# Keys and values of two groups by seven products, and transfers by one queue, in an attention and feed-forward kernel

## The chip, the cores and the metric

The kernel runs on one core of a Trainium2 chip. The core has five engines that work in parallel, each through its own list of instructions in order: PE (matrix products; its weight loads are shown apart as PEld), DVE (vector work), ACT (scalar functions and copies), POOL (general work) and SP (which here only issues transfers). SP, ACT and POOL can each issue DMA transfers. The metric is the device time of one execution in microseconds (us); lower is better. A profile is one execution recorded by the hardware.

## The reference

The input x has 1024 rows of 512. All arithmetic is float32. Two layers are computed, each as x + layernorm(f(layernorm(x))):

```python
# f of layer 1: causal attention, 32 query heads in 8 groups, head size 128
q = (xn @ w_q).reshape(B, S, 8, 4, 128)      # w_q: 512 x 4096
k = (xn @ w_k).reshape(B, S, 8, 128)         # w_k: 512 x 1024
v = (xn @ w_v).reshape(B, S, 8, 128)         # w_v: 512 x 1024
scores = einsum(q, k) * 128 ** -0.5          # causal mask
attn = softmax(scores) @ v                   # per head
out = attn.reshape(B, S, 4096) @ w_o         # w_o: 4096 x 512
# f of layer 2: a dense 512 x 512 product with bias, plus 8 low-rank experts (rank 16)
# weighted by a softmax router with 15 outputs
```

## The kernel before

**Tiling.** Group g has one key head, one value head and four query heads. A row t is 128 of the 1024 positions. A block (g, t) is one row of one group; its scores are four tiles of 128 lines, 4 heads x 32 positions each (`NSUB` is 4), against all positions up to its own. There are 64 blocks. The first 48 go group by group through rows 0 to 7. The last 16 alternate between groups 6 and 7 in pairs of rows 0-1, 6-7, 4-5, 2-3, so that a row's attention is complete there and its second layer can begin. In the text, (2..5, 2) means row 2 of groups 2 to 5, and (1, 3, 5; 7) row 7 of groups 1, 3 and 5. An index u counts pairs of rows (256 positions).

**One turn of the main loop (`for i in range(N)`)** does the following for block i:

- `loads(i)` issues weight loads that later blocks need. Before the change ACT issues them.
- For each of the four score tiles, `scores` runs one or two matmuls into a PSUM tile (`s`, two buffers), then mask (L519), maximum (L521) and exp with row sum (L526). One tile later follow the reciprocal (L532) and the scaling of the probabilities (L533), and then a DVE transpose of 32 x 32 pieces into `T` (L539).
- After the fourth tile `to_keys` moves `T` into `K` by 16 transfers, which put positions on partitions. By the remainder of a count by three, 11 go to SP and 5 to POOL.
- Between the tiles `run_share` spreads the block's other PE work: the query projection of a later pair of rows (odd i), key and value projections (`other`), `attend(i - 2)`, which multiplies the probabilities in `K` with the values (`po`), and for even i the output projection of an earlier pair of rows (`project_o_pair`: products a to e, then DVE accumulates at L640). `weave` mixes two lists in proportion to their columns. What stands first in a list runs first.

So block i's probabilities are transposed early in turn i + 1, transferred, and used in turn i + 2.

**Keys and values.** `project_k(g, qb)` computes 128 x 512 keys by four matmuls of 512 columns, and ACT evicts them with the factor `scale` (L359). It runs at rows 2 and 6. `project_v(gv, t)` computes the values of two groups for one row by four matmuls of 256 columns, ACT evicts them (L344), and it runs at every row of even groups.

**Seven products.** From the third pair of rows on the query projection (`project_q_halves`) and the output projection use a scheme after Strassen and Winograd: of a product of 2 x 2 blocks it needs seven block products instead of eight, on sums of the operands. `combine_q` makes the sums of the weights and `combine_x` those of xn, on POOL. A PSUM bank holds two to four products; `merge` adds banks into the result, one ACT copy and then DVE additions (L418). PSUM has three banks (`bank`) for all projections.

**Buffers that matter.** `wq` has one buffer, `wk`, `wv` and `wo` have two, `po` has one bank, attnT (the attended rows, evicted by ACT at L565) has three.

**The end.** After the loop the last rows are ordered by hand: `project_o_pair` of the last pair of group 6, `attend` and `project_o` of the last two blocks, and for the rows c, d, e, f the router and feed-forward pieces (`out_x[0]` and `out_x[2]` hold two base products each, `out_x[1]` a transpose, `out_x[3]` the last product). DVE's and ACT's order there is fixed by `go`.

Most instructions are marked to keep their place on their engine; the others (the merges among them) are placed by the scheduler. All matmuls carry the line of one helper (L102), all kept transfers that of another (L108), so that they are told apart by their tiles.

Of the kernel before, what the change touches and what calls it, by code (L numbers as in the profile page):

```python
# [15 lines left out]
P = 128  # L16
# [6 lines left out]
def kernel(  # L23
# [15 lines left out]
):  # L39

# [80 lines left out]

    def load_q(g, i, by=nc.scalar):

        if weights.get(("q", i), (None,))[0] == g:
            return
        hw = R * D // 2
        w = wp.tile([P, KC, hw], F32, tag=f"wq{i}", name=f"wq_{g}_{i}", bufs=1)
        load(w, w_q[:, ts(2 * g + i, hw)].rearrange("(c p) n -> p c n", p=P), by)
        weights["q", i] = (g, w)

    def combine_q(m):


        g = pairs[m][0]
        if weights.get("sq", (None,))[0] == g:
            return
        w = [weights["q", i][1] for i in range(2)]
        hk = KC // 2
        a11, a12, a21, a22 = w[0][:, :hk], w[0][:, hk:], w[1][:, :hk], w[1][:, hk:]
        s1, s2, s4 = (  # L140
            ffn.tile([P, hk, 2 * D], F32, tag="hy", name=f"sq_{g}_{n}", bufs=3) for n in range(3)
        )
# [7 lines left out]
        weights["sq", 0] = (a11, a12, s4, a22, s1, s2, a21)  # L150
        weights["sq"] = (g,)

    def combine_x(m):

        u = pairs[m][1]
# [3 lines left out]
        t12, t34 = (ffn.tile([P, 2, hk, P], F32, tag="x", name=f"tx_{m}_{n}") for n in range(2))  # L159
# [3 lines left out]
        weights["tx"] = (b11, b21, b22, t4, t1, t2, t3)  # L163

    def load_v(gv, i, by=nc.scalar):
# [4 lines left out]
        load(w, rows.rearrange("(c p) n -> p c n", p=P), by)  # L170
        for c in range(KC // 2):
            weights["v", gv, i * (KC // 2) + c] = w[:, c, :]
# [167 lines left out]

    def project_v(gv, t):
        def finish(pm):
            v = vs[gv, t] = act.tile([P, GV * D], F32, tag="v", name=f"v_{gv}_{t}", bufs=NT + 2)
# [11 lines left out]

    def project_k(g, qb):
        def finish(pm):
            kT = kTs[g, qb] = act.tile([P, QB], F32, tag="kT", name=f"kT_{g}_{qb}", bufs=2 * NQB)
            nc.scalar.mul(kT, pm, scale)  # L359
# [41 lines left out]

    def project_q_halves(m):
# [14 lines left out]
        def add(dst, src, to):  # L417
            nc.vector.tensor_tensor(dst, src, to, ALU.add)  # L418

        def merge(b):  # L420

            one, two = pm[b][:, 0], pm[b][:, 1]
            if b == 0:
                nc.scalar.copy(both(0), one.unsqueeze(1).to_broadcast([P, 2, NSUB, 2 * SQ]))  # L424
                add(half(0, 0), two, half(0, 0))
            elif b == 1:
                add(half(1, 0), one, half(0, 1))
                add(half(0, 1), two, half(1, 0))
            elif b == 2:
                add(half(1, 1), one, half(0, 1))  # L430
                add(half(1, 0), one, half(1, 0))
                add(half(1, 0), two, half(1, 0))
            else:
                add(half(0, 1), one, half(0, 1))


        order = (0, 1, 5, 6, 4, 2, 3)

        def piece(n, c, k):
            i, b, x = order[n], n // 2, n % 2  # L440
# [5 lines left out]
            assert weights["sq"] == (g,)  # L446
# [15 lines left out]
        ]  # L462

# [38 lines left out]
    def scores(g, t, j):  # L502
# [32 lines left out]
        def finish():  # L535
# [8 lines left out]
            if j == NSUB - 1:  # L544
                to_keys(g, t)
# [3 lines left out]
    def to_keys(g, t, by=(nc.sync, nc.sync, nc.gpsimd)):  # L549
# [9 lines left out]
    def weighted_values(g, t):  # L559


        def finish(po):
            o = act.tile([P, R * P], F32, tag="attnT", name=f"attnT_{g}_{t}", bufs=3)
# [172 lines left out]
    def ffn_out(t):  # L736
# [3 lines left out]
        def base(c):  # L740
            if c == 0:

                if t in (e, f):
# [3 lines left out]
            matmul(pf[0], state["hT", t][:, c, :], weights["base", c], start=(c == 0), stop=False)  # L747
# [23 lines left out]
        w = [(512, lambda c=c: base(c)) for c in range(KC)]  # L771
# [11 lines left out]
    def projections(i):  # L783
# [12 lines left out]
        if i < N2:  # L796
            if t == 2:
                other += project_k(g, 1)
            if t == 6:
# [4 lines left out]
            elif g % GV == 0 and (g or t >= TPB):  # L804
                other += project_v(g // GV, t)
        else:
            n = i - N2
            for k, what in ((0, (G - 1, 0)), (2, (G - 2, 1)), (3, (G - 1, 1))):
                if n == k:
                    other += project_k(*what)  # L810
# [207 lines left out]
```

## Time and profile before

| | |
|---|---|
| Runs | 1077.7, 1077.79, 1078.58 us; median 1077.79 |
| Profiled execution | 1077.89 us, of which the span from the first to the last instruction is 1076.1 |
| Granted clock of PE | 0.996 of full speed |
| Transfers T to K | 11 x 64 on SP, 5 x 64 on POOL |

A line of the groups gives source line, engine, operation, output<-inputs, shape and count; then busy time in us, mean ns of one, and the idle time ahead of them with what ended it. A line of the timeline gives start and duration in us, engine, line, operation and count; a bracket holds the wait before it. A line of the windows gives the stretch, its length, and the busy time and number of instructions of PE, PEld, DVE, ACT and POOL, then the clock and the DMA.

### The profile page before, as it was taken

What the parts mean: (1) busy time and instruction counts of PE and PEld (TensorE: products, weight loads), DVE (VectorE), ACT (ScalarE), POOL (GpSimd) and SP (SyncE); (2) the same over time, 40 slices, a digit from 0 to 9 for tenths busy, and PEclk for the clock granted to TensorE, in tenths of its full rate; (3) what the DMA queues carried; (4) which work ended last, traced back from release to release, by engine and by line L of the source; (5) the groups of instructions that cost most, each with busy time, mean ns of one, the idle gap of its engine ahead of it and who ended that gap; (6) DMA issues with size and microseconds to landing.
All of it is one profiled execution on the core that took longest, in us unless ns stands there. A gap on an engine that the chain in (4) does not pass through costs nothing.

```text
span 1076.1 us, 15090 instructions
## 1 busy us (share of the span) xinstructions
PE 1053.7 (98%) x4398; PEld 708.9 (66%) x4398; DVE 703.5 (65%) x1689; ACT 480.9 (45%) x969; POOL 360.7 (34%) x720
## 2 busy tenths in 40 slices
PE   9999999999999999999999999999999999999995
PEld 7776666667676676766777676756676566466442
DVE  4586657876576657866576666877337676576756
ACT  2654435544354434544354434554235454353411
POOL 2734245243333335332352334332142122232412
PEclk9999999999999999999999999999999999999998
DMA  5244242553135432454124531545334555343221
GB/s 186 50 129 117 69 120 68 161 141 89 33 86 145 94 89 59 128 140 123 33 74 133 127 87 46 141 130 129 77 108 118 159 139 133 108 117 100 69 69 39
DMA packets 74913, 111.96 MB, mean 104 GB/s; under 512 B 18176, under 2 KB 47760, under 8 KB 74832
## 3 DMA queue, kind: packets, MB, share of 16 engines
q1 hardware_dynamic: 38576, 59.29, 21.9%
q0 software_dynamic: 11216, 24.45, 9.2%
q10 hardware_dynamic: 25040, 27.27, 8.0%
q8 instruction: 36, 0.59, 0.2%
q14 instruction: 45, 0.37, 0.1%
HBM read 33.34 MB, written 2.10 MB: 33 GB/s over the span
## 4 chain that ended last, share of the span: by engine, by line
PE 89%; DVE 5%; POOL 2%; DMA 1%; ACT 1%; issue 1%; SPq 1%; POOLq 0%; ACTq 0%; DVEq 0%
PE po L102 21%; PE s L102 21%; PE pq L102 17%; PE pv L102 5%; PE pk L102 5%; PE pa L102 4%; PE pe L102 4%; PE pO L102 2%; PE pb L102 2%; PE pd L102 2%; PE pc L102 2%; PE pf L102 2%; SPq L108 1%; DVE T L539 1%; POOL K L108 1%
## 5 line engine op out<-in xcount | busy, mean ns | idle before, releaser
L533 ACT ACTIVATE p<-p,rec 128x32 f32<-128x32 f32 (+31 forms) x256 | 188.1, 735 | 225.0 <-DVE rec L532 160.4
L102 PE MATMUL po<-K,v 128*128 128x512 f32 x576 | 279.2, 594 | 2.4 <-DMA K<-T 2.1
L102 PE MATMUL s<-kT,qT 128*128 128x512 f32 (+15 forms) x768 | 272.5, 464 | 3.8 <-ACT attnT L565 2.1
L526 ACT ACTIVATE p<-s,nmax 128x32 f32<-128x32 f32 (+31 forms) x256 | 179.1, 700 | 189.6 <-DVE nmax L521 180.6
L108 POOL DMA_DIRECT2D K<-T x320 | 157.9, 500 | 265.0 <-DVE s L519 55.1
L539 DVE STREAM_TRANSPOSE T<-p 128x128 f32<-128x128 f32 (+7 forms) x256 | 197.6, 773 | 64.8 <-ACT p L533 54.2
L102 PEld LDWEIGHTS s<-kT,qT 128*128 128x128 f32 x768 | 141.4, 190 | 127.1 <-issue 107.2
L521 DVE TENSOR_REDUCE nmax<-s 128x1 f32<-128x32 f32 (+31 forms) x256 | 180.6, 705 | 7.7
L102 PEld LDWEIGHTS po<-K,v 128*128 128x128 f32 x576 | 104.8, 190 | 64.3 <-issue 54.1
L519 DVE TENSOR_TENSOR s<-s,smask 128x32 f32<-128x32 f32 x256 | 48.2, 188 | 112.5 <-PE s L102 112.0
L102 PE MATMUL pq<-xnT,wq 128*128 128x128 f32 (+1 forms) x656 | 113.8, 321 | 0.0
L102 PEld LDWEIGHTS pq<-xnT,wq 128*128 128x128 f32 x656 | 100.6, 191 | 14.7 <-issue 7.7
L524 POOL MEMSET p<- 128x96 f32 (+2 forms) x192 | 29.9, 161 | 235.6 <-DVE T L539 198.0
L418 DVE TENSOR_TENSOR qT<-pq,qT 128x256 f32<-128x256 f32 x161 | 63.4, 413 | 34.8 <-ACT qT L424 27.2
L102 PE MATMUL pv<-wv,xnT 128*128 128x256 f32 x256 | 71.2, 381 | 0.5 <-ACT xnT L293 0.5
L565 ACT COPY attnT<-po 128x512 f32<-128x512 f32 x64 | 37.3, 582 | 66.7 <-PE po L102 66.4
L102 PE MATMUL pk<-xnT,wk 128*128 128x512 f32 x128 | 64.5, 593 | 0.0
L102 PE MATMUL pa<-wo,attnT 128*128 128x256 f32 x224 | 61.8, 385 | 0.0
L162 POOL TENSOR_TENSOR tx<-xnT 128x256 f32<-128x256 f32 x46 | 33.4, 726 | 81.1 <-PE pq L102 74.3
L102 PEld LDWEIGHTS pq<-tx,wq 128*128 128x128 f32 x368 | 49.6, 192 | 9.1 <-issue 7.7
L102 PEld LDWEIGHTS pq<-tx,sq 128*128 128x128 f32 x368 | 49.8, 192 | 8.6 <-issue 8.3
L102 PEld LDWEIGHTS pa<-wo,attnT 128*128 128x128 f32 x224 | 41.2, 190 | 19.2 <-issue 14.3
(121 smaller groups left out, 1165.1 us busy)
## 6 DMA issues: line engine op xcount, KB each, us to landing
wq<-in_w_q_dram ACTq DMA_DIRECT2D x27, 512.0 KB, 5.0
K<-T SPq DMA_DIRECT2D x88, 128.0 KB, 3.6
K<-T SPq DMA_DIRECT2D x88, 112.0 KB, 3.3
K<-T SPq DMA_DIRECT2D x88, 96.0 KB, 2.6
wo<-in_w_o_dram ACTq DMA_DIRECT2D x28, 256.0 KB, 3.9
K<-T SPq DMA_DIRECT2D x88, 80.0 KB, 2.7
K<-T SPq DMA_DIRECT2D x88, 64.0 KB, 2.2
K<-T POOLq DMA_DIRECT2D x40, 128.0 KB, 4.6
```

Source lines behind the costliest of these rows:

```text
L102: keep(nc.tensor.matmul(*args, **kw))
L108: keep(by.dma_start(dst, src))
L162: nc.gpsimd.tensor_tensor(dst, p, q, ALU.subtract)
L418: nc.vector.tensor_tensor(dst, src, to, ALU.add)
L519: keep(nc.vector.tensor_tensor(s[:, n - SQ : n], s[:, n - SQ : n], smask, ALU.add))
L521: keep(nc.vector.tensor_reduce(nmax, s[:, :n], AX.X, ALU.max, negate=True))
L524: nc.gpsimd.memset(p[:, n:full], 0.0)
L526: keep(nc.scalar.activation(p[:, :n], s[:, :n], AF.Exp, bias=nmax, accum_out=total))
L533: keep(nc.scalar.mul(p[:, :n], p[:, :n], rec))
L539: nc.vector.transpose(turned[g, t][:, :, j, :, :].rearrange("p b k q -> p k b q"), p[:, :full].rearrange("p (k b q) -> p k b q", b=R, q=SQ),)
L565: copy = nc.scalar.copy(o, po)
```

## The change

- `combine_w` takes the sums out of `combine_q`. `combine_k` and `combine_v` use it for two groups at once, and `project_halves` computes keys and values of groups 2 to 7 by seven products per 256 positions: each product is two matmuls of 128 columns, one bank holds four products, and `merge` has one ACT copy and six DVE additions. Groups 0 and 1 keep the old way. The xn sums of `combine_x` are used by keys, queries and values of the same rows.
- They run in odd turns, keys before the queries and values after. The last three of groups 6 and 7 run in turns 49 to 51, with `combine_x` at the end of the turn before.
- `scale` is multiplied into w_k by ACT (`scale_k`) two rows after it is loaded, instead of into the keys.
- The query products come in the order 0, 1, 5, 6, 3, 2, 4 instead of 0, 1, 5, 6, 4, 2, 3; the last merge is one addition of 512.
- All weight loads in the loop are issued by SP. All 16 transfers of a block are issued by SP, but for the first block, rows 1 to 3 of groups 1, 3 and 5, and the last block, which keep 11 and 5.
- attnT has two buffers. Values of two rows share a tile, keys have four tiles by name.
- At the end `project_o_pair` and the base products of row c come first, then `attend(N - 2)`; `attend(N - 1)` moves behind `project_o(N - 2)`.

```diff
+    def scale_k(g):
+        keep(nc.scalar.mul(weights["k", g], weights["k", g], scale))
...
+    def combine_w(key, parts, sums):
+        (a11, a12, a21, a22), (s1, s2, s4) = parts, sums
         for dst, p, q, op in (
             (s1, a21, a22, ALU.add),
             (s2, s1, a11, ALU.subtract),
...
+        weights[key] = (a11, a12, s4, a22, s1, s2, a21)
...
     def project_k(g, qb):
         def finish(pm):
-            kT = kTs[g, qb] = act.tile([P, QB], F32, tag="kT", name=f"kT_{g}_{qb}", bufs=2 * NQB)
-            nc.scalar.mul(kT, pm, scale)
+            nc.scalar.copy(key_tile(g, qb), pm)
...
+    PRODUCTS = (0, 1, 5, 6, 3, 2, 4)
...
             if b == 0:
-                nc.scalar.copy(both(0), one.unsqueeze(1).to_broadcast([P, 2, NSUB, 2 * SQ]))
+                q = each(0).rearrange("p (e s) n -> p e s n", e=2)
+                nc.scalar.copy(q, one.unsqueeze(1).to_broadcast([P, 2, NSUB, 2 * SQ]))
                 add(half(0, 0), two, half(0, 0))
             elif b == 1:
-                add(half(1, 0), one, half(0, 1))
-                add(half(0, 1), two, half(1, 0))
+                add(half(1, 0), one, half(1, 0))
+                add(half(1, 1), two, half(1, 0))
             elif b == 2:
-                add(half(1, 1), one, half(0, 1))
-                add(half(1, 0), one, half(1, 0))
+                add(half(0, 1), one, half(1, 1))
                 add(half(1, 0), two, half(1, 0))
             else:
-                add(half(0, 1), one, half(0, 1))
-        order = (0, 1, 5, 6, 4, 2, 3)
+                add(both(1), one.unsqueeze(1).to_broadcast([P, 2, NSUB, 2 * SQ]), both(1))
...
+    def project_halves(name, u, sums, product, quarters):
+        hk = KC // 2
+        pm, to = {}, {}
+        def merge(b):
+            c11, c12, c21, c22, first = to[0]
+            p = pm[b]
+            if b == 0:
+                nc.scalar.copy(first, p[:, 0:1, :].to_broadcast([P, 2, P]))
+                add(first, p[:, 1:3, :], first)
+                add(c22, p[:, 3], c12)
+            else:
+                add(c21, p[:, 0], c22)
+                add(c12, p[:, 1], c12)
+                add(c12, p[:, 2], c12)
+                add(c22, p[:, 2], c22)
+        def piece(n, k):
+            i, b = PRODUCTS[n], n // 4
...
+            lhsT, rhs = product(weights[sums][i][:, k, :], weights["tx"][i][:, k, :])
+            matmul(pm[b][:, n % 4, :], lhsT, rhs, start=(k == 0), stop=(k == hk - 1))
+            if k == hk - 1 and n in (3, 6):
+                merge(b)
+        return [(P, lambda n=n, k=k: piece(n, k)) for n in range(7) for k in range(hk)]
...
             if j == NSUB - 1:
-                to_keys(g, t)
+                three = (nc.sync, nc.sync, nc.gpsimd)
+                at = blocks.index((g, t))
+                short = at < 1 or at < N2 and g % 2 and t in (1, 2, 3)
+                alone = not short and at < N - 1
+                to_keys(g, t, by=three[:1] if alone else three)
...
-            o = act.tile([P, R * P], F32, tag="attnT", name=f"attnT_{g}_{t}", bufs=3)
+            o = act.tile([P, R * P], F32, tag="attnT", name=f"attnT_{g}_{t}")
...
+        if i % 2 and m < len(pairs) and n < 0:
+            gm, um = pairs[m]
+            if gm >= first and gm % 2 == 0:
+                q = project_k_halves(gm, um) + q + project_v_halves(gm // GV, um)
...
+        elif 0 < n < NT // 2:
+            q = project_k_halves(G - 2, n) + q
+            other += project_v_halves((G - 2) // GV, n)
         return q, other
     def loads(i):
         g, t = blocks[i]
+        by = nc.sync
...
     rescale_scores()
+    o_pair = project_o_pair(*pairs[N // 2 - 2])
     finish_scores()
...
-    o_pair = project_o_pair(*pairs[N // 2 - 2])
-    run([turn_d] + weave(o_pair[:8], attend(N - 2)) + [products_d] + o_pair[8:])
+    run(o_pair[:8] + out_c[0] + out_c[2] + o_pair[8:16] + [turn_d] + o_pair[16:])
+    run(attend(N - 2) + [products_d])
     go(d)
-    run(out_c[0] + out_c[1] + out_c[2] + attend(N - 1))
-    run(project_o(*blocks[N - 2]))
+    run(out_c[1] + project_o(*blocks[N - 2]))
     go(e)
     run(out_c[3])
     go(e, e)
-    run(project_o(*blocks[N - 1]))
+    run(attend(N - 1) + project_o(*blocks[N - 1]))
```

## The prediction

> **What bounds the kernel.** The page's first two parts come first: one engine is busy almost throughout, and the chain that ended last runs through it.
>
> ```profile
> PE 1053.7 (98%) x4398; PEld 708.9 (66%) x4398; DVE 703.5 (65%) x1689; ACT 480.9 (45%) x969; POOL 360.7 (34%) x720
> ...
> PE 89%; DVE 5%; POOL 2%; DMA 1%; ACT 1%; issue 1%; SPq 1%; POOLq 0%; ACTq 0%; DVEq 0%
> ```
>
> So a microsecond of PE work is worth a microsecond, wherever PE does not begin to wait instead. Next, the groups by shape: the key and value projections that the change replaces, the query products that are already done in seven parts, and two DVE additions that resemble the new ones.
>
> ```profile
> L102 PE MATMUL pv<-wv,xnT 128*128 128x256 f32 x256 | 71.2, 381 | 0.5 <-ACT xnT L293 0.5
> L102 PE MATMUL pk<-xnT,wk 128*128 128x512 f32 x128 | 64.5, 593 | 0.0
> L102 PE MATMUL pq<-tx,wq 128*128 128x128 f32 x368 | 53.3, 275 | 0.0
> L418 DVE TENSOR_TENSOR qT<-pq,qT 128x256 f32<-128x256 f32 x161 | 63.4, 413 | 34.8 <-ACT qT L424 27.2 <-PE pq L102 6.2
> L726 DVE TENSOR_TENSOR hw<-pl,w 128x128 f32<-128x128 f32 x8 | 2.3, 289 | 0.2
> ```
>
> Every float32 matmul leaves two records: 4 groups of values x 8 rows x 4 pieces make 128 matmuls and 256 records. I call a record a pass. Passes overlap, so a mean of 381 ns is no price; the price is the step from start to start in the timeline.
>
> ```profile
> 17.38 3.60 PE L102 MATMUL pk<-xnT,wk 128*128 128x512 f32 x8
> 20.81 3.62 PE L102 MATMUL pq<-xnT,wq 128*128 128x256 f32 x16
> ...
> 510.03 1.95 PE L102 MATMUL pq<-xnT,wq 128*128 128x128 f32 x16
> 511.81 1.06 PE L102 MATMUL pq<-tx,sq 128*128 128x128 f32 x8
> ```
>
> 8 passes of 512 columns take 20.81 - 17.38 = 3.43 us, 0.429 each; 16 of 256 take 3.46 (the next group starts at 24.27), 0.216 each; 16 of 128 take 1.78, 0.112 each. The price per column is nearly the same for all three.
>
> **1. The products, on the path.** For a pair of groups the keys were 2 x 2 x 4 = 16 matmuls of 512, 32 passes x 0.429 = 13.73 us; the values 64 passes x 0.216 = 13.82. Both become 4 x 7 x 2 = 56 matmuls of 128, 112 passes x 0.112 = 12.54. A pair saves 1.19 + 1.28 = 2.47 us, three pairs 7.4.
>
> Here a page speaks against the change. The Trainium skill (TensorE: Matmul & The Clock Gate, "Back-to-back issue gap") says that in a stream of weight loads and matmuls the load counts too, and gives about 81 ns for 128 columns against 131 for 512: four short ones would cost 2.5 times one long one. By that ratio 112 short passes cost as much as 112 x 0.429 x 81/131 = 29.7 us where the row says 12.54, and the three pairs would lose some 95 us. The row is float32, of the same shape and in the same place, with a weight load before each pass, so I take 0.112.
>
> **2. Where the work moves.** By counting each block's passes in the instruction order of the changed kernel (a block is a group and a row, a score matmul begins it), blocks (2..5, 2) fall to 9.17 us of PE work, from 12.60 in odd groups and 14.33 in even ones; (2..5, 6) and (1, 6) lose 3.4 to 5.2. Blocks (2, 4; 1, 3, 5) gain 4.5, and (1, 3, 5; 7) gain 6.3. PE's sum stays -7.4, but an engine that was hidden under 12.6 us must now fit into 9.2.
>
> **3. DVE.** A merge of four quarters adds one addition of 256 (0.413) and five of 128 (0.289 each): 1.86 us. 24 merges are 44.6, less 3 for queries (23 x one 256-wide addition, about 0.14 saved when two become one of 512). They stand where PE got 4.5 to 6.3 us more, and are hidden there. The critical block is (3, 2), where DVE has lost nothing:
>
> ```profile
> 407.50:418.60 11.10, 11.10 (x43) 7.61 (x42) 8.44 (x23) 5.79 (x14) 3.53 (x9) 1.00 0.19 48
> ...
> 184.00:197.10 13.10, 13.10 (x55) 9.08 (x54) 11.33 (x33) 6.90 (x13) 2.93 (x8) 1.00 0.41 106
> ```
>
> Columns: length, busy PE, weight loads, DVE, ACT, POOL. DVE's 8.44 against 9.17 is a share of 0.92; the highest that I find without a PE stall is 11.33 of 13.10, 0.865. At 0.865 the block takes 9.8 us: 0.6 lost, in four groups 2.4. From nothing (two score tiles of slack) to 2.4; I take 1.5.
>
> **4. Order of the query products.** In odd groups a score matmul waits for the last query merge (0.9 us at block (g, 3), 0.4 at (g, 5), each three times). The last merge is now 512 wide, 0.69 by the row of the same width (acc<-pd), instead of 0.41: at (g, 5) 0.3 later, three times, +0.9. At (g, 3) two additions after the last product replace three: even. In even groups value products follow and hide it.
>
> **5. Transfers.** SP issues 16 of 16 per block instead of 11; the other five go to POOL in 11 blocks only.
>
> ```profile
> 342.32 0.97 DVE L539 STREAM_TRANSPOSE T<-p 128x768 f32<-128x768 f32 x1
> ...
> 343.36 7.35 SPq L108 DMA_DIRECT2D K<-T  x11
> ...
> 366.92 1.02 PE L102 MATMUL po<-K,v 128*128 128x512 f32 x2
> ...
> 1012.57 21.55 SPq L108 DMA_DIRECT2D K<-T  x22
> ```
>
> This is block (2, 5): transposed at 343.3, 11 transfers issued in 7.35, 0.64 from one to the next where none waits (7.0 in most blocks), used at 366.92: 23.6 us of time. Sixteen need 15 x 0.64 + 2.6 for the last to land (the page's median for 96 KB) = 12.2. But (2, 6) loses 5.2 us, and in (2, 7) the products with K move forward by 6.2 because the four value projections ahead of them in the woven list are gone: 12.2 us remain, no margin. The same count leaves 0.1 at (4, 5), -0.1 at (6, 3), and 1.1 to 1.9 at ten more blocks: (1, 3, 5; 4), (1, 3, 5; 5), (2, 4; 1), (2, 4; 3); 1.7 at (3, 5; 1), which keep three queues; elsewhere over 2. I take +1.0 for three places with none, from 0 to +4.
>
> The second page that bears on it: the Trainium skill (DMA: Bandwidth & Descriptors, "Issuing engines are not separate DMA queues") says that several issuing engines save only the issue time, usually small beside the transfer. By that the five transfers cost SP next to nothing. The row says 0.64 us each, 3.2 us of delay per block, as much as the landing itself (2.6). I count the row.
>
> Weight loads, 71 issues, go from ACT to SP. They stand ahead of the block's transfers, are issued when SP has just done the previous block's, and wait for products already finished: 0.5 us each, four at most, with the transpose still 4 us away. If the cover went, K would be 2 us late. ACT and POOL are freed of about 30 and 130 us, neither on the path: a gain of 0 to 2 (two early stalls of 0.6 and 0.9 with late POOL work near them); I take 0. Scaling w_k: 8 x 0.6 on ACT, well ahead of use; POOL's sums: 36 x 0.73 (24 for weights, 12 for xn), in blocks where it loses nearly as much in transfers; the closest, xn's for block (7, 1), come some 2.2 us after their tile is free and are needed after 2.9. Nothing for both. attnT with two buffers instead of three: its old content is read before the new is copied, nothing.
>
> **6. The end.** PE waits before the last blocks:
>
> ```profile
> 1021.10 1.10 PE L102 MATMUL po<-K,v 128*128 128x512 f32 x2 [1.88 <-DMA K<-T]
> ...
> 1024.22 1.13 PE L102 MATMUL pb<-wot,sums 128*128 128x256 f32 x4 [0.30 <-DVE acc L640]
> ...
> 1028.43 1.25 PE L102 MATMUL pl<-ra_sb,hT 128*128 128x143 f32 x8 [1.36 <-ACT hT L293]
> ```
>
> With waits not bracketed there, 4.9 us in all. The new order puts the output pair first, so K of (7, 2) is in time and hT too. But pb needs DVE's sums, which come at 1022.3 when pa ended at 1019.9: a new wait of 2.4. Then pb, pc 1.75, base products 3.43, pd, pe 2.6, a transpose 0.45, po 2.6, pl and ptw 1.2, pO 3.4, pf 0.9 lead to 1038.6; K of (7, 3), transposed near 1027.9 behind three accumulations, is there at 1036.8; po 3.4, the copy 0.65, pO 3.4 end at 1046.2 against 1047.4 before. From there the work is unchanged and PE fills it. Gain 1.2; bounds -3.7 (the wait for sums gone) to +1.
>
> **Sum.** -7.4 + 1.5 + 0.9 + 1.0 - 1.2 = -5.2. The profiled execution took 1077.89 us with a span of 1076.1; the median of the runs is 1077.79. Span 1070.9, median **1072.6 us**, 0.5% less.
>
> **Rivals.** (a) SP decides, slower. If one issue costs not 0.64 but 0.80 us (8.7 for 11 at (2, 7), when transfers wait for earlier ones to land), sixteen end 2.4 us later; over the thirteen places the stalls are 13 x 2.4 - 14.9 (sum of the margins) = 16 us, and the time 1072.6 - 1.0 + 16 = 1088. It breaks even at 13x - 14.9 = 6.2, x = 1.6 us or 0.75 per issue. Against it: the slow issues stood beside POOL's transfers, which are gone. (b) DVE paces (g, 2) to (g, 5). At its share over these four blocks in group 3, 41.2 us of 52.1 = 0.79, their length stays as it was, and 2 x 3.4 us of the gain is lost: 1072.6 - 1.5 + 6.9 = 1078. Against it: the 0.865 above. (c) The covers hold, POOL's and ACT's relief takes the early stalls and the sums at the end come in time: -7.4 - 2 - 3.7 + 0.9 = -12.2, 1065.6. (d) That it doesn't do what it says is excluded for counts: the changed order holds 336 short matmuls and 55 transfers on POOL.
>
> **Numbers.** Forecast 0.62, (a) 0.12, (b) 0.12, (c) 0.14. The forecast's own range is 1069 to 1076; with (c) below and (b) above, and the bounds of steps 3 and 5, 1066 to 1079.5. A measurement of this kernel tells 0.2%, 2.2 us, from no change. Faster: 0.58 of the forecast + (c) + a little of (b) = 0.74; same 0.12; slower 0.14.
>
> **What would show it.** Right: pk and pv with 336 passes each of 128 columns beside what is left of the old shapes, in 0.112 steps; PE busy down by about 7; DVE up by some 40. Step 3 shows as waits of PE's s at (g, 2); step 5 as waits of po for DMA K<-T at the thirteen blocks; step 6 as pb waiting for sums near 1020 and no wait for K. It is wrong if those waits sum to more than 6 us, or if passes of 128 step slower than 0.112 where keys and values stand together.

## The result

The changed kernel took 1066.36 us in the median (1065.36 to 1067.22), the kernel before 1078.18 beside it: a ratio of 0.9889, with a 95% interval from 0.9872 to 0.9907, so 11.8 us less in the medians, and 12.0 by the ratio (10.0 to 13.8). The forecast was 1072.6, 5.2 us less: the direction was right, the gain was more than double. Its profiled execution took 1066.64 us with a span of 1064.9, 11.2 less than the span before. The page of after, its lines for the engines, the chain and K's largest transfers:

```profile
PE 1046.5 (98%) x4782; PEld 729.8 (69%) x4782; DVE 740.1 (70%) x1810; ACT 480.7 (45%) x965; POOL 255.0 (24%) x491
...
PE 90%; DVE 3%; SPq 3%; ACT 1%; DMA 1%; issue 1%; POOL 0%; POOLq 0%; DVEq 0%; ACTq 0%
...
K<-T SPq DMA_DIRECT2D x128, 128.0 KB, 2.4
```

PE is busy 7.2 us less, DVE 36.6 more, POOL 105.7 less; the chain still runs through PE. K's transfers of 128 KB now land after 2.4 us in the median; the page of before had 3.6:

```profile
K<-T SPq DMA_DIRECT2D x88, 128.0 KB, 3.6
```

The groups by shape, after (line, engine, operation, tiles, shape and count, then busy time and mean):

```profile
L103 PE MATMUL pk<-xnT,wk 128*128 128x512 f32 x32 | 15.7, 592 | 0.0
L103 PE MATMUL pk<-tx,sk 128*128 128x128 f32 x96 | 14.6, 275 | 0.0
L103 PE MATMUL pv<-sv,tx 128*128 128x128 f32 x96 | 15.6, 275 | 0.0
L450 DVE TENSOR_TENSOR qT<-pq,qT 128x512 f32<-128x512 f32 x23 | 15.8, 686 | 2.1 <-PE pq L103 0.2
L450 DVE TENSOR_TENSOR kT<-pk,kT 128x128 f32<-128x128 f32 x60 | 15.2, 287 | 3.1 <-PE pk L103 1.7
```

And the timeline of PE where keys come in short passes:

```profile
294.62 0.61 PE L103 MATMUL pk<-tx,sk 128*128 128x128 f32 x4
295.06 1.06 PE L103 MATMUL pk<-tx,wk 128*128 128x128 f32 x8
295.96 0.61 PE L103 MATMUL pk<-xnT,skv 128*128 128x128 f32 x4
```

Eight passes take 295.96 - 295.06 = 0.90 us, 0.1125 each: step 1's price, and not the page's ratio that was weighed against it.

The longest waits of PE after the start of the program, in the changed kernel (us in all, how often, the longest):

```profile
PE s L103 <- ACT p L625: 1.3, 4, 0.3
PE pb L103 <- DVE top L817: 1.1, 1, 1.1
PE po L103 <- DMA wo<-in_w_o_dram: 1.0, 2, 0.5
PE pc L103 <- DVE rec L631: 1.0, 1, 1.0
PE pO L103 <- ACT attnT L669: 0.7, 1, 0.7
PE po L103 <- DMA K<-T: 0.5, 1, 0.5
```

The two waits of po that the profile puts down to w_o's load stand before the first product with K of (2, 3) and (4, 3); SP issues w_o right behind that K. pb and pc are the second and third product of the output projection.

These lines give the part that the profile counts as idle. To account for the whole span I give each pass the usual step from start to start of its width (0.429 us for 512 columns, 0.216 for 256, 0.112 for 128, and so on) and call what a step takes beyond it waiting. Passes, waiting, the tail and 1.5 us ahead of the first pass make the span. Groups 1 to 5 are taken from 130 to 745 us, the end from 1005. The runs are those of the next section.

| Kernel | Passes | Waiting of PE | of it, groups 1 to 5 | of it, the end | Last pass to end of program | Span |
|---|---|---|---|---|---|---|
| before | 1044.7 | 18.0 | 5.4 | 6.1 | 11.8 | 1076.1 |
| products alone (b_kv) | 1037.3 | 24.0 | 6.4 | 6.6 | 11.8 | 1074.7 |
| the four other parts (b_all4) | 1044.7 | 12.3 | 2.1 | 4.0 | 9.7 | 1068.2 |
| after | 1037.4 | 16.3 | 6.1 | 3.9 | 9.7 | 1064.9 |
| after, one copy moved (a_copykeep) | 1037.3 | 14.0 | 3.3 | 3.9 | 9.7 | 1062.6 |

So of 11.2 us 7.4 are passes, as forecast. The other 3.8 are waits that went, less those that came, and 2.1 us behind the last pass, which the forecast had no term for.

### The profile page after: what moved, and what is told of

Its sections match the earlier page's. It is cut to its first block, busy times and chain, and to the rows that moved or that the text cites. A ratio compares the mean times of both kernels' runs of the same rounds, so it can differ in the third digit from the quotient of the medians.

```text
span 1064.9 us, 15423 instructions
## 1 busy us (share of the span) xinstructions
PE 1046.5 (98%) x4782; PEld 729.8 (69%) x4782; DVE 740.1 (70%) x1810; ACT 480.7 (45%) x965; POOL 255.0 (24%) x491
## 4 chain that ended last, share of the span: by engine, by line
PE 90%; DVE 3%; SPq 3%; ACT 1%; DMA 1%; issue 1%; POOL 0%; POOLq 0%; DVEq 0%; ACTq 0%
PE po L103 22%; PE s L103 20%; PE pq L103 19%; PE pv L103 5%; PE pe L103 4%; PE pa L103 4%; PE pk L103 4%; PE pf L103 3%; PE pO L103 3%; SPq L109 3%; PE pc L103 2%; PE pb L103 2%; PE pd L103 2%; PE pl L103 1%; DMA wo<-in_w_o_dram 1%
## 5 line engine op out<-in xcount | busy, mean ns | idle before, releaser
L188 POOL TENSOR_TENSOR tx<-xnT 128x256 f32<-128x256 f32 x52 | 37.9, 729 | 209.8 <-PE pv L103 124.6
L103 PE MATMUL pa<-wo,attnT 128*128 128x256 f32 x224 | 58.8, 385 | 0.0
L103 PEld LDWEIGHTS pq<-tx,wq 128*128 128x128 f32 x368 | 47.1, 192 | 7.6 <-issue 7.5
L103 PEld LDWEIGHTS pq<-tx,sq 128*128 128x128 f32 x368 | 47.5, 192 | 5.7 <-issue 5.0
L103 PE MATMUL pq<-tx,sq 128*128 128x128 f32 x368 | 51.2, 275 | 0.0
L625 ACT ACTIVATION_READ_ACCUMULATOR p<-s,nmax 128x1 f32 x256 | 49.5, 193 | 0.0
L103 PE MATMUL pq<-tx,wq 128*128 128x128 f32 x368 | 49.2, 275 | 0.0
```

The lines of the kernel that those rows point to most:

```text
L103: keep(nc.tensor.matmul(*args, **kw))
L188: nc.gpsimd.tensor_tensor(dst, p, q, ALU.subtract)
L625: keep(nc.scalar.activation(p[:, :n], s[:, :n], AF.Exp, bias=nmax, accum_out=total))
```

## Experiments

My theory after this comparison: step 1 is right, and the rest of the gain comes from the other parts, through the order of the query products, through POOL's freedom, and through the end. The rivals are the forecast's own steps (each part costs 1 us or nothing) and that the products took waits with them. Differences in us are (ratio - 1) x 1078, against the kernel before of the same comparison; the changed kernel stands at -12.0 in this measure (-10.0 to -13.8). The name in brackets is that of the run: b_ starts from the kernel before, a_ from the changed one.

### Each part alone in the kernel before

Transfers by SP alone (b_alone). To `to_keys` of before:

```
-                to_keys(g, t)
+                at = blocks.index((g, t))
+                short = at < 1 or at < N2 and g % 2 and t in (1, 2, 3)
+                alone = not short and at < N - 1
+                to_keys(g, t, by=three[:1] if alone else three)
```

> The kernel before, with the rule of the change for K's transfers alone: 53 of 64 blocks by SP only. The products stay as they were. By step 5 of the prediction this costs: five more issues of 0.64 us per block, +3.2 us until K lands, in blocks that still have 2 to 6 us of margin here because no product has moved: 0 to +1 us. The rival (c), relief: POOL no longer issues beside its own work and each K lands sooner (the page of after has 2.4 us for 128 KB instead of 3.6), so -1 to -4 us, and the waits of PE's s at (g, 3) and (g, 5) shrink if they came from POOL. A third theory concerns the end of the program: POOL's last drain took 7.85 us in the trace of before and 5.98 in that of after; if the number of POOL's transfers sets it, it takes about 6 here and the time falls by 1.9 us from that alone.

Measured: ratio 1.0024 (1.0013 to 1.0035), +2.6 us. PE's timeline at the end of this kernel:

```profile
1024.26 2.04 PE L102 MATMUL po<-K,v 128*128 128x512 f32 x2 [5.34 <-DMA K<-T]
```

It was 1.88 there: 3.5 us more, near step 5's price of five more issues (5 x 0.64 = 3.2). And the two passes behind it take 2.04 us instead of 1.02: the granted clock from 1024.0 to 1028.5 is 0.50. Against this, POOL's last drain (the DRAIN instruction at the end of its list) fell from 7.85 to 5.98 us, as the third theory had it.

Weight loads by SP (b_spload): `load_q`, `load_k`, `load_v`, `load_o`, `load_base` of the loop get `nc.sync`.

> The kernel before, with the weight loads of the main loop issued by SP instead of ACT (71 issues). The prediction counted 0 (bounds 0 to -2). Rival: the waits of PE's s for q or ACT's p at (g, 3) and (g, 5), 4.1 us in all, came from ACT standing in its load issues; then -2 to -4 us and these waits are gone. If neither, 0 within 1 us and the same waits.

Measured: 1.0039 (1.0026 to 1.0051), +4.2 us. Neither theory. PE waits of pc, three times about 1.0 us, stand where DVE is late; POOL and DVE ahead of one of them, from the timeline:

```profile
338.02 1.26 POOL L149 TENSOR_TENSOR sq<-wq 128x512 f32<-128x512 f32 x1 [0.79 <-DMA wq<-in_w_q_dram]
339.37 1.27 POOL L149 TENSOR_TENSOR sq<-sq,wq 128x512 f32<-128x512 f32 x1
339.49 1.43 DVE L616 TENSOR_TENSOR sums<-attnT 128x256 f32<-128x256 f32 x1 [1.62 <-ACT attnT L565]
340.95 1.37 DVE L617 TENSOR_TENSOR sums<-sums,attnT 128x256 f32<-128x256 f32 x1
342.25 1.48 DVE L618 TENSOR_TENSOR attnT<-attnT,attnT 128x256 f32<-128x256 f32 x1
343.65 0.41 DVE L619 TENSOR_TENSOR sums<-attnT,sums 128x256 f32<-128x256 f32 x1
```

Three of DVE's four additions take 1.4 us, and 0.42 elsewhere. SP brings wq sooner, so that POOL's four sums begin at 338.0 instead of 344.7 and fall on them. The Trainium skill (SBUF — State Buffer, "SBUF: two separate sides") says that a DVE operation with two inputs from SBUF and a GpSimd (POOL) operation that reads SBUF exclude each other for a whole instruction; these rows agree, with 1.0 us for each. The test moves POOL's sums out of the way (b_spload_late):

```
-            if i % 2 == 0 and n < 2 and i // 2 + 1 in QW:
-                (combine_x, combine_q)[n](i // 2 + 1)
+            if i % 2 == 0 and n in (0, 3) and i // 2 + 1 in QW:
+                (combine_x if n == 0 else combine_q)(i // 2 + 1)
```

> The kernel before with weight loads by SP (as in the run that cost 4.2 us), and POOL's four sums of the query weights given out after the block's last score tile instead of the second. There wq landed earlier, and POOL's sums (338.0 to 343.4) fell on DVE's four sums of attnT, which took 1.43, 1.37, 1.48 and 0.41 us instead of 0.42 each; pc then waited 1.0 us. If that collision is the cost, the long additions and the waits of pc are gone and the time is that of before within 1 us; if SP's loads themselves are the cost, it stays at +4 us.

Measured: 0.9981 (0.9973 to 0.9989), -2.0 us. The long additions and the waits of pc are gone. The collision was the cost. Without it the loads by SP and the later sums together gain 2.0 us: PE's waiting up to 130 us is 4.1 us (5.6 before). That is where step 5 had seen early stalls and had named a relief of 0 to -2; that it comes from ACT rather than from POOL's later sums is likely, not shown.

The order of the query products (b_qorder, `PRODUCTS` with its merges). What s waited for in the kernel before, at (g, 3), (g, 5) and once in group 0:

```profile
PE s L102 <- ACT attnT L565: 2.1, 3, 0.7
PE s L102 <- DVE qT L418: 1.2, 4, 0.7
```

> The kernel before, with the new order of the seven query products and its merges alone. The prediction's step 4: +0.9 us, because the last addition is 512 wide (0.69 us instead of 0.41) at (g, 5), three times, and (g, 3) stays even. Rival: the new order is what removed the waits at (g, 3) (0.95 each, three times) and (g, 5) (0.42 each, three times), because the last half of q that the first score product needs is written earlier or by fewer DVE instructions: -3 to -4 us.

Measured: 0.9973 (0.9965 to 0.9980), -2.9 us. The waits of s at (g, 3) and (g, 5) are gone, and one at the end came back 1.0 us longer. The timeline of before, at the end of block (3, 3):

```profile
427.97 1.02 PE L102 MATMUL po<-K,v 128*128 128x512 f32 x2
428.84 1.05 DVE L418 TENSOR_TENSOR qT<-pq,qT 128x256 f32<-128x256 f32 x3
429.70 1.24 PE L102 MATMUL s<-kT,qT 128*128 128x512 f32 x4 [0.71 <-ACT attnT L565]
```

and of after at the same place:

```profile
426.62 1.02 PE L103 MATMUL po<-K,v 128*128 128x512 f32 x2
427.48 1.16 PE L103 MATMUL s<-kT,qT 128*128 128x512 f32 x4
427.49 1.18 DVE L450 TENSOR_TENSOR qT<-pq,qT 128x256 f32<-128x256 f32 x2
```

Before, s begins when the last additions are nearly done (the releaser that the profile names is an eviction that ended at the same time). After, s begins together with the additions and waits for nothing. They end no sooner and one is wider; but s does not read what they write. In the old order the last product goes into the part of q of the pair's first row, `half(0, 1)`, which the next block's score products read at once. In the new order that part is complete after the product before, and the last merge writes `both(1)`, the second row, needed a block later.

To separate this from the width I put product 3 last (a_qrow0), with the same number of additions of the same widths:

```
-            i, b, x = PRODUCTS[n], n // 2, n % 2
+            i, b, x = (0, 1, 5, 6, 2, 4, 3)[n], n // 2, n % 2
...
-                add(both(1), one.unsqueeze(1).to_broadcast([P, 2, NSUB, 2 * SQ]), both(1))
+                add(half(0, 1), one, half(1, 1))
+                two = pm[2][:, 1]
+                add(both(1), two.unsqueeze(1).to_broadcast([P, 2, NSUB, 2 * SQ]), both(1))
```

> The changed kernel with query products 2 and 4 ahead of 3. There are as many additions of the same widths; but the part of q that belongs to the first row of the pair, which the next block's score products read at once, is written after the last product, and not, as in the change, before it. Theory of step 4 (the width of the last addition, 512 or 256, sets the wait): no change against the changed kernel, 1066 to 1067. Theory from the traces (what counts is which row the last merge writes; the change made it the second row's, needed a block later): the waits of s at (g, 3) and (g, 5) of groups 1, 3 and 5 return, about 0.8 to 1 us and 0.4 us each, +2.5 to +4 us.

Measured: 0.9919 (0.9906 to 0.9933), -8.7 us, 3.2 us above the changed kernel. The timeline of this kernel:

```profile
429.67 1.11 DVE L450 TENSOR_TENSOR qT<-pq,qT 128x256 f32<-128x256 f32 x2
430.19 1.24 PE L103 MATMUL s<-kT,qT 128*128 128x512 f32 x4 [0.38 <-DVE qT L450]
```

The waits are back: 0.54 us at (1, 3), (3, 3) and (5, 3), 0.35 at (3, 5) and (5, 5), and 2.2 at one place in group 0, behind which the clock was low. (K's waits at (2, 3) and (4, 3) shrank by 0.5 each in return, since PE came later.) s begins about 0.1 us after the first addition, 256 wide, has ended, and doesn't wait for the second, 512 wide. The row that is written decides, not the width. It is this timeline that shows it; of the 3.2 us in all, the place in group 0 and the low clock behind it are a large part.

The end alone (b_end):

> The kernel before, with the new order of the last rows alone. The prediction's step 6: -1.2 us (-3.7 to +1), with pb waiting 2.4 us for DVE's sums. The comparison of the two traces has waits before the last output product of 4.9 us before and about 3.0 after, so -1.9 if the order alone did it; 0 if the earlier landing of K (SP alone) did it.

Measured: 0.9998 (0.9990 to 1.0006), no difference. The K wait went, as step 6 had it, and pb waited as forecast. PE's timeline:

```profile
1021.96 1.84 PE L102 MATMUL pb<-wot,sums 128*128 128x256 f32 x4 [2.20 <-DVE pr L711]
1023.59 2.04 PE L102 MATMUL pc<-wot,attnT 128*128 128x256 f32 x4
```

Four passes of 256 take 1.63 us here, start to start, instead of 0.86. The windows of this kernel (length, PE, weight loads, DVE, ACT, POOL, granted clock, DMA share, GB/s):

```profile
1021.70:1025.30 3.60, 3.34 (x8) 2.45 (x9) 2.96 (x11) 0.00 (x0) 0.00 (x0) 0.57 0.00 0
1026.00:1030.00 4.00, 4.00 (x13) 2.22 (x12) 1.70 (x6) 1.53 (x2) 1.01 (x2) 1.00 0.07 15
```

The clock is 0.57 for 3.6 us after the wait. So the wait of 2.4 us cost about 1.7 more, and the new order's gain was used up.

The products alone (b_kv; with w_k scaled and two buffers of attnT):

> The kernel before with the seven products for keys and values alone (with the scaling of w_k and two buffers of attnT); transfers, weight loads, query order and end as before. By step 1 -7.4 us for the passes, and by step 3 +1.5 to +2.4, so -5 to -6. From the difference of the changed kernel and the one with the four other parts (-4.6 us): about -3 to -5. If POOL's sums for keys and values collide with its transfers, which here it still issues, less.

Measured: 0.9994 (0.9986 to 1.0002), -0.6 us, no difference that can be told. The five parts alone add up to +3.1 us; together they gave -12.0. In the table the passes are 7.4 us less and the waits 6.0 more. Of these, 3.4 stand at one place, (7, 6), of which the timeline shows ACT and PE:

```profile
853.90 0.58 ACT L671 COPY attnT<-po 128x512 f32<-128x512 f32 x1 [7.40 <-PE po L103]
854.38 0.99 ACT L634 ACTIVATE p<-p,rec 128x832 f32<-128x832 f32 x1
855.27 0.97 ACT L627 ACTIVATE p<-s,nmax 128x864 f32<-128x864 f32 x1
...
856.39 1.12 PE L103 MATMUL s<-kT,qT 128*128 128x512 f32 x2 [2.52 <-ACT p L627]
```

ACT stood for 7.4 us at the copy of po, with two ready operations behind it, and s waited for the second. This copy isn't pinned; the scheduler put it ahead of this exp here, and behind it in the kernel before, where ACT waited 5.05 us at the same copy and PE did not. The test (b_kv_pin) holds the copy in program order at (7, 6) and at (2..5, 2):

```
-            if held:
+            if held or t == 0 and 2 <= g < G - 2 or (g, t) == (G - 2, 6):
                 keep(copy)
```

> The products alone, as before, with ACT's copy of attnT held in program order, behind the exps, at (2..5, 2) and at (7, 6). If ACT's order is what ate the products' gain (4 x 0.6 us, and at (7, 6) 2.7 + 0.7 us and what follows), the waits go and the time is 6 to 7 us under before: the passes of step 1 in full. If the products' gain is lost otherwise (DVE's share of step 3, POOL's sums), the waits appear elsewhere and it stays above -3 us.

Measured: 0.9941 (0.9928 to 0.9953), -6.4 us (-5.1 to -7.8). The products are worth their passes as soon as ACT's order lets them.

So two of the five single runs carry an accident of the order: in b_spload 6.2 us that b_spload_late takes away, and in b_kv 5.7 us, of which the changed kernel keeps only the 2.3 at (2..5, 2). Of the 15.1 us between the sum of the single runs and the whole, these two are 9.6. By this estimate some 5.5 are left for parts that help each other; most of that is likely the end of the program (a_endold in the next section).

### The four other parts together, and each part taken out

The four other parts together (b_all4):

> The kernel before with four parts of the change together: transfers by SP alone, weight loads by SP, the new query order and the new end; keys and values still by the old products. If step 1 was right (-7.4 us for the products, nothing else from them), this kernel is 7 to 8 us above the changed one, 1073.5 to 1074.5, some 4 us under before. If the products brought more than their passes (waits that went with them), it is above 1075; if the four parts brought more than the sum of what each brings alone (+2.6 +4.2 -2.9 0 = +3.9 us), which they must if step 1 was right, then it lies under before although the sum says 1081.6.

Measured: 0.9932 (0.9919 to 0.9946), -7.3 us. Above 1075 was excluded, and so was the sum of the single runs; 7 to 8 us above the changed kernel did not come either. The sum is missed by 11.2 us. Of these 6.2 are the collision of b_spload, which this kernel doesn't have; most of the rest is likely that the new end gains beside SP alone (a_endold, below) what it doesn't gain by itself (b_end). With the changed kernel this leaves about 4.6 us to the products (3.3 in the spans): 7.4 of passes less 4.0 of new waits.

The old order of the query products (a_qold):

> The changed kernel with the old order and merges of the query products. Step 4 of the prediction: -0.9 us. The reading of the run with the new order alone (-2.9 us, waits of s at (g, 3) and (g, 5) gone): +2.5 to +4 us, and these waits are back at groups 1, 3 and 5.

Measured: 0.9918 (0.9904 to 0.9931), 3.1 us above the changed kernel; the waits are back.

K's transfers shared again (a_three):

> The changed kernel with every block's K transfers shared, 11 by SP and 5 by POOL, as before. Step 5 of the prediction: -1.0 us (0 to -4), because SP has 3.2 us less to issue. Rival: POOL's drain at the end of the program is back at 7.85 us (5.98 now), and K lands later because POOL's own transfers land late: +1.9 us from the drain, and up to +2 more where POOL's sums for keys and values stand ahead of its transfers.

Measured: 0.9927 (0.9914 to 0.9939), 4.1 us above the changed kernel. The drain is 7.85 us again, and pb waits 2.37 us instead of 1.27. The timeline of POOL in this run:

```profile
1005.85 2.51 POOL L109 DMA_DIRECT2D K<-T  x5 [0.54 <-PE s L103]
1008.37 0.56 POOL L294 TENSOR_TENSOR rstd_h<-ve_h,neg_half 128x1 f32<-128x1 f32 x1
```

and of after:

```profile
1006.53 0.55 POOL L294 TENSOR_TENSOR rstd_h<-ve_h,neg_half 128x1 f32<-128x1 f32 x1 [1.05 <-DVE rec L631]
```

A norm's small operation stands behind five transfers; DVE's normalisation waits for it, the sums of pb come 1.1 us later, and then the clock falls too (0.57 from 1014.6 to 1018.4). This was the relief of POOL that step 5 counted at nothing. Before 130 us PE waits 1.7 us more in this run, where POOL's and DVE's additions meet again (three of DVE's take 1.37 to 1.48 us); in groups 1 to 5 it waits 1.8 us less, since K of (2, 3) and (4, 3) is in time.

The old end (a_endold):

> The changed kernel with the old order of the last rows. Step 6 of the prediction: +1.2 us (-1 to +3.7). The run of SP alone with the old end had one wait of 5.3 us for K at the end; if it is back here, +3 to +5 us: the new order's worth is then that it covers SP's longer issue, not the waits that the old kernel had.

Measured: 0.9931 (0.9919 to 0.9943), 4.5 us above. A wait of 5.1 us for K is back, with the slow clock behind it. The new order pays for SP's longer issue; with the old sharing it gained nothing.

### Steps 3 and 5

Four waits of s, 0.6 us each, appeared at (2..5, 2), where step 3 expected them from DVE. The timeline of after:

```profile
288.75 0.48 DVE L620 TENSOR_REDUCE nmax<-s 128x1 f32<-128x320 f32 x1
289.39 0.59 ACT L669 COPY attnT<-po 128x512 f32<-128x512 f32 x1 [0.71 <-PE po L103]
289.87 0.53 ACT L625 ACTIVATE p<-s,nmax 128x320 f32<-128x320 f32 x1
290.55 0.59 PE L103 MATMUL s<-kT,qT 128*128 128x384 f32 x1 [0.33 <-ACT p L625]
```

DVE's maximum is there at 289.23. ACT first waits for po and copies it. The test (a_copykeep) holds this copy in program order:

```
-            if held:
+            if held or t == 0 and 2 <= g < G - 2:
                 keep(copy)
```

> The changed kernel with ACT's eviction of po (attnT) at blocks (2..5, 2) behind the exp of the next two score tiles instead of ahead of them. Step 3 (DVE paces these blocks): the four waits of 0.6 us stay, 0. Theory from the timeline: DVE's maximum was there at 289.23, but ACT first waited for po and copied it until 289.98, so ACT's order makes the wait; then the four waits go, -2.4 us, or -1 if DVE then takes over as the limit.

Measured: 0.9868 (0.9855 to 0.9882), 1064.08 us, 2.3 us under the changed kernel, and the fastest run that computes everything. The two intervals overlap; what decides is the trace, in which the four waits, 2.3 us, are gone. The timeline at the same place:

```profile
289.05 0.48 DVE L620 TENSOR_REDUCE nmax<-s 128x1 f32<-128x320 f32 x1
289.62 0.53 ACT L625 ACTIVATE p<-s,nmax 128x320 f32<-128x320 f32 x1 [0.65 <-DVE nmax L620]
290.35 0.85 PE L103 MATMUL s<-kT,qT 128*128 128x384 f32 x2
...
292.26 0.58 ACT L669 COPY attnT<-po 128x512 f32<-128x512 f32 x1
```

The same work on DVE, and no wait: ACT's order made it.

DVE relieved of the mask in these blocks (a_masked, `if t != 2 or g < 2 or g >= G - 2:` ahead of the addition):

> The changed kernel without DVE's addition of the mask in blocks (2..5, 2), which leaves out that part of the computation: DVE has 4 x 0.19 us less in each. Step 3 (DVE paces): the waits of s at (2..5, 2) fall from 0.6 to 0.2 us, -1.5 us in all. ACT's order: they stay at 0.6 us, 0.

Measured: 0.9864 (0.9851 to 0.9878), -14.7 us. The waits went here as well, but this run tells nothing apart: with less on DVE the scheduler also put the exp ahead of the copy.

K was late at (2, 3) and (4, 3), by 0.79 and 0.73 us. Two runs move w_o, first to ACT at the same row (a_woact, `load_o(g + 1, nc.scalar)`), then on SP to row 6 for even groups (a_wo6, `if t == (5 if g % 2 else 6)`):

> The changed kernel with the loads of w_o in the loop (4 of 256 KB at row 5) issued by ACT again. Step 5 as predicted: the lateness at (2, 3) and (4, 3), 0.79 and 0.73 us in the trace, comes from SP's sixteen issues alone, and stays: 0. Theory from the trace: the last of K's sixteen transfers, issued 0.7 us before w_o's first, shares the engines with w_o's 256 KB and lands 3.2 us after its issue instead of 2.0; then the two waits go, -1.5 us, and if w_o's issue by ACT holds up ACT's exp, less.

Measured: 0.9938 (0.9925 to 0.9952), 5.3 us above the changed kernel. The waits grew to 2.2 and 1.4 us, and behind the first the clock was 0.54 for 3.5 us. ACT issues w_o at 322.9 to 324.8, among K's last transfers, where SP did so behind them. Neither expectation held. The last transfer of K at (2, 3) took 5.2 us from issue to landing here and 3.6 in the changed kernel, where 2.0 is usual for this size; so w_o beside K does make it later, as the second theory has it.

> The changed kernel with w_o of the odd groups loaded one block later (row 6 of the even groups instead of row 5), still by SP. If w_o's 256 KB transfers beside K's last transfer make K late at (2, 3) and (4, 3), the waits of 0.79 and 0.73 us go and no other comes, since K of row 4 has over 2 us of margin: -1.5 us. If SP's sixteen issues alone make K late (step 5), the waits stay.

Measured: 0.9928 (0.9915 to 0.9940), 4.2 us above the changed kernel. 0.4 and 0.6 us of the waits stay without w_o there, so w_o's bytes are the smaller part. K's last transfer still takes 3.3 and 3.6 us there, and what holds it no run shows. What made the kernel slower is seen in the next run as well.

The next run (a_best) gives five of the sixteen transfers of (2, 3) and (4, 3) to POOL again, on top of the moved copy:

```
-                short = at < 1 or at < N2 and g % 2 and t in (1, 2, 3)
+                short = at < 1 or at < N2 and (g % 2 and t in (1, 2, 3) or g in (2, 4) and t == 3)
```

> The changed kernel with ACT's copy of attnT behind the exps at (2..5, 2), which took 2.3 us, and K of (2, 3) and (4, 3) shared 11 to 5 with POOL. If SP's five more issues (3.2 us, step 5) make K late there, the waits of 0.79 and 0.73 us go, and the time is 1.5 us under that of the copy alone, some 1062.5. If the lateness comes from w_o's bytes, they stay at 0.3 us or more; if POOL's sums of xn hold its transfers up, they grow.

Measured: 0.9900 (0.9885 to 0.9915), 3.4 us above a_copykeep. The two waits are gone, so SP's five issues are their larger cause. But the timeline of this kernel at (2, 6) shows the collision again:

```profile
344.42 1.31 DVE L720 TENSOR_TENSOR sums<-attnT 128x256 f32<-128x256 f32 x1 [1.32 <-ACT attnT L669]
345.53 1.34 POOL L145 TENSOR_TENSOR sq<-sq,wq 128x512 f32<-128x512 f32 x1
345.77 1.38 DVE L721 TENSOR_TENSOR sums<-sums,attnT 128x256 f32<-128x256 f32 x1
```

DVE's four sums take 1.31 to 1.49 us, here and in a_wo6. The instruction order of both kernels shows why: the scheduler moved one memset of p, which waits for DVE, from ahead of POOL's sums of the weights to behind them; in the changed kernel it keeps POOL until 349.5. DVE, late by 4 us, makes s wait 0.83 us and K of row 5 come 0.8 to 1.1 us late in these two kernels; in the changed kernel K of that row had landed 2.5 us before its use. The drain took 6.79 us.

All transfers by SP (a_nopool, `by=three[:1]`):

> The changed kernel with all K transfers by SP, also those of the first block, of rows 1 to 3 of groups 1, 3 and 5 and of the last. POOL's drain took 7.85 us with 320 transfers of POOL and 5.98 with 55. If it is in proportion to the number, it takes 5.6 here and nothing is gained; if it waits for something that only a queue in use has, it falls well under 5, and the end of the program comes up to 1.2 us sooner (then SP's own end decides). By step 5 the blocks (3, 5; 1) had a margin of 1.7 us with three queues, of which 3.2 us are used: 0 to +3 us for K that is late at rows 1 to 3.

Measured: 0.9999 (0.9990 to 1.0008), all of the gain lost. K of rows 1 to 3 of the odd groups is late by up to 3.2 us; PE waits 12.6 us more in all, 10.7 of them in groups 1 to 5, so the exceptions are worth that. The drain took 1.48 us.

## Why the prediction was wrong, by its steps

Two steps failed, both in their sign. Step 4 charged 0.9 us for a wider last addition, where the new order takes 4.1 us of waits away. Step 5 charged 1.0 us for transfers by SP and put the relief of POOL at nothing, where SP alone is worth 4.1 us to the changed kernel.

- **What bounds the kernel, step 1 (-7.4).** Right, to 0.1 us: 1044.7 of passes became 1037.4, at 0.112 each.
- **Step 3 (+1.5).** 2.4, the upper bound that was given, at the four places named. The reason was wrong, and that the size fits is luck. I read DVE's share of 0.92 as a limit; PE waited for an exp that ACT held behind a copy. The step compared busy shares and didn't look at the order on the engine that hands over.
- **Step 4 (+0.9).** This step failed: "The last merge is now 512 wide, 0.69 ... instead of 0.41". The 4.1 us of waits at (g, 3) and (g, 5), which the trace of before shows, went altogether. I priced how long the last addition takes and never asked which half of q it writes; the diff says it, `half(0, 1)` before, `both(1)` after. That is a swing of 5.0 us, of the 6.0 by which the forecast of the span was wrong; the order as a whole measured 2.9 alone and 3.1 taken out, since other waits grow where these go, so by the runs alone the swing is some 4.
- **Step 5 (+1.0).** This step failed too. Its cost was sized well: 1.5 us for K that is late, and 0.64 per issue, since five more took 3.5 us at the end of b_alone. The places differ: (2, 3) and (4, 3), to which I had given 1.1 to 1.9 of margin, were late; at (2, 5) and (4, 5), to which I had given none, K landed 2.5 us before its use, and only (6, 3) had nothing to spare (0.2). What failed is the other side of the sum: for the relief of ACT and POOL "I take 0". POOL's relief took 1.1 us from pb and kept the clock up, worth about another 1.7, and a term was missing: the drain, -1.9.
- **Step 6 (-1.2).** About -2.2. pb waited 1.3 and not 2.4, by POOL's relief. As written it would have cost more than forecast, since 2.4 us of waiting brought another 1.7 at the lower clock (b_end).
- **Sum.** -7.4 + 2.4 - 4.1 + 1.5 - 2.2 - 2.1 (drain 1.9, the rest of the tail 0.2) = -11.9, and 0.7 of small waits elsewhere make the -11.2 of the spans. Rival (c) named two mechanisms that came, relief and the sums at the end nearer in time, and 1065.6. That its number is so near is in good part luck: the early stalls, of which it took 2 us, fell by 0.2 (5.6 us of waiting before 130 us, then 5.3), its +0.9 for step 4 had the wrong sign too, and it had neither the drain nor late K.

## What to carry to other kernels

For a merge or any last step ahead of a consumer, ask which bytes the consumer reads first before pricing how long the step takes. A part tested alone can carry an accident of the order that the whole does not have, and parts that look independent can be each other's cover: here five parts gave +3.1 us one by one and -12.0 together, and accidents made 9.6 of the 15.1 us between the two. So test each part by taking it out of the whole as well, and read the trace of each single run before adding it up. Where a scheduler places evictions on an in-order engine, look at each edit for a copy that has moved ahead of a ready exp; one pinned line was worth 2.3 us here and 5.7 in b_kv; and for two engines' additions that have moved onto each other.

## What the runs showed of the hardware

- POOL's last DRAIN grows with the number of transfers that POOL has issued in the whole program, though they had landed long before. The longest of POOL's three, in before and after (min, median and max in ns):

```profile
L1014 POOLq DRAIN  x3: 46/102/7852, 1067.4 to 1075.8; - x3
L1138 POOLq DRAIN  x3: 46/102/5976, 1058.1 to 1064.6; - x3
```

  Its length in the trace, for all runs alike with the same number:

| Transfers issued by POOL | 6 | 61 | 71 | 326 |
|---|---|---|---|---|
| Drain, us | 1.48 | 5.98 | 6.79 | 7.85 |

  From 6 to 71 that is 0.082 us each; up to 326 it grows by only 1.06 more, so by this estimate there is a limit somewhere near 84, if the slope holds until then. Each K transfer is 32 to 34 packets on POOL's queue, so transfers and packets can't be told apart here. What the drain does in this time no run shows.
- After some waits of PE the granted clock was 0.50: for 3.4 us after waits of 2.2 (twice), 2.4 (twice) and 3.2 us, and for 6.8 us after 5.1 and 5.5 us (a_endold, b_alone), the end of these longer waits included. After 2.0, 2.6 and 2.7 us (before at 1021, a_nopool at 436, b_kv at 856) it stayed at 1.00. So no fixed length decides. The Trainium skill (TensorE: Matmul & The Clock Gate, "Why this matters for your kernels") warns of gaps of over some 3 us; here 2.2 were enough, at a price of about 2 us each where it was reckoned (1.7 in b_end, 1.9 in a_qrow0).
- Additions of POOL and DVE with their inputs in SBUF, at the same time, cost DVE 0.9 to 1.1 us for each of its 0.42 us instructions (b_spload, a_wo6, a_best, a_three).
- SP's transfers of 128 KB landed in 3.6 us where POOL issued five of each sixteen (before), and in 2.4 where SP issued all sixteen of most blocks (b_alone, after).
